# Attention's keys in four column groups, and the first queries' maxima in four row groups between the projections

## The chip, the cores and the metric

The kernel runs on one core of one Trainium2 chip, in one launch. The metric is the device time of that core in microseconds (us). Several executions are timed, and their median counts; one further execution is recorded by the hardware profiler, and every duration below comes from that one.

The core has five engines with queues of their own: PE multiplies matrices into PSUM, DVE and ACT work on vectors (ACT evaluates functions from tables that it has to load), POOL does slower vector work, and SP issues DMAs. They wait for each other through semaphores, and each takes its own instructions in order.

## What is computed

Four images of 256 channels and 64x64 pixels go through four layers, each on a group normalisation `_gn` of the running x and added back to it:

```
x = x + layer0(_gn(x))   # deformable 3x3 convolution
x = x + layer1(_gn(x))   # attention
x = x + layer2(_gn(x))   # deformable convolution, 16 groups
x = x + layer3(_gn(x))   # state-space (scan) layer
```

The change lies in layer 1:

```
q = xf @ Wq.T + bq            # 4096 pixels x 32
k = xf @ Wk.T + bk            # 4096 pixels x 32
v = relu(xf @ Wv.T + bv)      # 4096 pixels x 128
attn = softmax(einsum('bnc,bmc->bnm', q, k), axis=-1)
comb = einsum('bnm,bmd->bnd', attn, v) @ Wc.T + bc
out = concatenate([comb, v], axis=-1)
```

## The kernel before

The images are worked on one after the other, and the four layers of an image too; x stays in SBUF as two tiles of 128 channels by 4096 pixels (`x[:, 0]` and `x[:, 1]`). `layer1` works on chunks of 512 pixels (`NCH` is 8) and on tiles of 128.

First `scaled` writes the normalised x, `xn`, in sixteen pieces on DVE (L186), two for each chunk. Its statistics need a square root on ACT (L175), with a table load ahead of it.

Then comes the part that I call the opening. For every chunk j it projects values, keys and queries (L496 to L501; the weights of queries and keys are held four times side by side, so that a projection gives the same 32 numbers in all four groups of 32 partitions). A projection is two fp32 matmuls, for the two halves of the channels, and every fp32 matmul leaves two records in the profile. DVE makes v from pv (bias and relu, `vt`, L503). ACT copies 32 partitions of pk to `ka` (L505): chunk j goes to partitions 32(j % 4) on, columns 512(j // 4) on. ACT also copies pq to `qa` (L506). PE transposes vt in four pieces (L509), and ACT copies the result to `v` (L510). DVE adds vt to `x[:, 1]` (L516) and takes its statistics for the next layer (`note`, L152).

The softmax subtracts each query's maximum, which `greatest` (L441) finds ahead for a block of 512 queries. It is a generator. A block has 32 products of 128 queries with 512 keys: a query tile t, a key column block c and a partition group g, each over 32 rows of PE. It does n of them at a time as a unit, into n PSUM banks (L455), and one DVE instruction takes the maxima of the n (L465); then it yields. After the last unit it reduces to one maximum for each query (L468), splits that into three bf16 parts on ACT and DVE (L472 to L475), and yields; when it is called again it turns them with four matmuls (pmt, L479) and copies the rows to `mr` (L483), which `scores` needs.

For the first block, n is 2, and two buffers of two banks are used (L489). The opening calls the generator four times at the end of every odd chunk (L512 to L514), so two key chunks have just become ready, and 16 units stand in four bursts of four. The last two calls (L518 and L519) stand after the loop. For the other seven blocks n is 3, and units stand between the products of attention.

After the opening come 64 steps of attention. `scores` (L523) multiplies keys and queries for 4x128 keys and 512 queries in four row groups, adds the negative maxima with bf16 products (L531), and ACT takes the exponential (`e`, L544); POOL sums e (L546, L548) and `weigh` multiplies it with v (L555). `scores(0)` stands ahead of the first step. Its four PSUM banks (`l1s`) use the room that the opening's four banks `l1p` had.

The order on PE is written by hand (`manual_schedule`); on DVE, ACT and POOL the framework's scheduler orders the instructions, and it also puts in the waits. A later step of the build puts in ACT's table loads.

Of the kernel before, what the change touches and what calls it, by code (L numbers as in the profile page):

```python
# [9 lines left out]
F32 = mybir.dt.float32  # L10
I32 = mybir.dt.int32
BF16 = mybir.dt.bfloat16
AF = mybir.ActivationFunctionType
ALU = mybir.AluOpType
AX = mybir.AxisListType

P = 128
# [46 lines left out]
class Net:  # L64
# [346 lines left out]
    def layer1(self, x):  # L411


        nc, tc = self.nc, self.tc
        KT = NT // 4
        with tc.tile_pool(name="l1a", bufs=1) as pa, tc.tile_pool(name="l1b", bufs=2) as pb:
            xn = pa.tile([P, 2, N], F32, tag="xn1", name="xn1")
# [7 lines left out]
            wq, wk, wv, wc, bq, bk, bv, bc = self.l1w  # L425
            qa = pa.tile([P, N], F32, tag="qa", name="qa")
            ka = pa.tile([P, N // 4], F32, tag="ka", name="ka")
            v = pa.tile([P, NT, P], F32, tag="v", name="v")
# [12 lines left out]
            def greatest(qb, wide, n):  # L441


                m8 = pb.tile([P, 4, 8], F32, tag="m8", name="m8")
                m = m8.rearrange("p t m -> p (t m)")
                if n == 2:
                    units = [(t, c, g) for c in range(2) for h in range(2) for t in range(4) for g in (2 * h, 2 * h + 1)]
                else:
                    units = [(t, c, g) for t in range(4) for c in range(2) for g in range(4)]
                for u in range(0, 32, n):  # L450
                    now = units[u : u + n]
                    sc = wide("pm")
                    for i, (t, c, g) in enumerate(now):
                        r = slice(32 * g, 32 * g + 32)
                        nc.tensor.matmul(  # L455
                            sc[:, i, :],
                            qa[r, bass.ts(4 * qb + t, P)],
                            ka[r, bass.ts(c, 512)],
                            start=True,
                            stop=True,  # L460
                            tile_position=(32 * g, 0),
                        )
                    t, c, g = now[0]
                    at = 8 * t + 4 * c + g
                    nc.vector.tensor_reduce(m[:, at : at + len(now)], sc[:, : len(now), :], AX.X, ALU.max)  # L465
                    yield
                mx = pb.tile([P, 4], F32, tag="mx", name="mx")
                nc.vector.tensor_reduce(mx, m8, AX.X, ALU.max, negate=True)  # L468
                mp = parts[qb % 2]
                for i in range(3):  # L470
                    t3 = pb.tile([P, 4], BF16, tag="t3", name="t3")
                    nc.scalar.copy(t3, mx)  # L472
                    nc.scalar.copy(mp[:, :, :, i], t3.rearrange("p (t u) -> p t u", u=1).to_broadcast([P, 4, 4]))
                    if i < 2:
                        nc.vector.tensor_sub(mx, mx, t3)  # L475
                yield
                pt = wide("pmt")[:, 0, :]
                for t in range(4):
                    nc.tensor.matmul(  # L479
                        pt[:, bass.ts(t, P)], mp[:, t].rearrange("p g r -> p (g r)"), identb, start=True, stop=True  # L480
                    )
                mr = pb.tile([P, 512], BF16, tag="mr", name="mr")
                nc.vector.tensor_copy(mr, pt)  # L483
                rows.append(mr)

            with (
                tc.manual_schedule(engines={mybir.EngineType.PE}),
                self.banks(4, "l1p") as pone,
                self.banks(2, "l1w") as ptwo,  # L489
            ):  # L490
                pair = lambda name: ptwo.tile([P, 2, 512], F32, tag="pm", name=name)
                one = lambda name: pone.tile([P, 512], F32, tag="p", name=name)
                ahead = greatest(0, pair, 2)
                for j in range(NCH):
                    to = {}
                    for n, w in (("v", wv), ("k", wk), ("q", wq)):  # L496
                        to[n] = one("p" + n)
                        for ct in range(2):
                            nc.tensor.matmul(
                                to[n], w[:, ct, :], xn[:, ct, bass.ts(j, 512)], start=(ct == 0), stop=(ct == 1)  # L500
                            )  # L501
                    vt = pb.tile([P, 512], F32, tag="vt1", name="vt1")
                    nc.vector.tensor_scalar(vt, to["v"], bv, 0.0, ALU.add, ALU.max)  # L503
                    r = slice(32 * (j % 4), 32 * (j % 4) + 32)
                    nc.scalar.activation(ka[r, bass.ts(j // 4, 512)], to["k"][r, :], AF.Identity, bias=bk[r])  # L505
                    nc.scalar.activation(qa[:, bass.ts(j, 512)], to["q"], AF.Identity, bias=bq)  # L506
                    pt = one("pvt")
                    for i in range(4):
                        nc.tensor.transpose(pt[:, bass.ts(i, P)], vt[:, bass.ts(i, P)], self.ident)  # L509
                    nc.scalar.copy(v[:, 4 * j : 4 * j + 4, :].rearrange("p t c -> p (t c)"), pt)  # L510

                    if j % 2:  # L512
                        for _ in range(4):
                            next(ahead)  # L514
                    xs = x[:, 1, bass.ts(j, 512)]
                    nc.vector.tensor_add(xs, xs, vt)  # L516
                    self.note(x, 1, j)
                next(ahead)  # L518
                next(ahead, None)  # L519

            blocks = [{} for _ in range(NCH)]
# [82 lines left out]
            with (  # L604
                tc.manual_schedule(engines={mybir.EngineType.PE}),
                self.banks(1, "l1s") as pscore,
                self.banks(1, "l1m") as pwide,
                self.banks(1) as self.psum,
            ):

                def wide(name):
                    return pwide.tile([P, 3, 512], F32, tag="wide", name=name)

                scores(0)
                ahead = itertools.chain(*(greatest(qb, wide, 3) for qb in range(1, NCH)))
                steps = 0
                for s in range(NCH * KT):
                    qb, kt = s // KT, s % KT
                    e = blocks[qb]["e"]
                    if s + 1 < NCH * KT:  # L620
                        scores(s + 1)

                    for i in range(4):
                        if steps < 4 + 12 * (s + (i + 1) / 4) / KT:
                            next(ahead, None)
                            steps += 1
                        weigh(s, e[i // 2], i)
                    if qb and kt in (1, 2, 3):
                        (divide, spread, combine)[kt - 1](qb - 1)
                for do in (divide, spread, combine):  # L630
                    do(NCH - 1)
# [901 lines left out]
```

## Time and profile before

| | |
|---|---|
| median of 3 runs | 10302.39 us (10298.44 to 10305.17) |
| the profiled execution | 10256.01 us |
| its span in the trace | 10254.2 us |
| PE, DVE, POOL, ACT busy | 86%, 77%, 64%, 47% of the span |
| granted PE clock, mean | 0.957 |
| first image: first pv to the first e (L544) | 613.43 to 691.65 us |
| second image | 3165.61 to 3244.07 us |
| third image | 5705.30 to 5783.68 us |
| fourth image | 8247.20 to 8323.72 us |
| in 613.4 to 691.0 busy: PE, DVE, ACT, POOL | 72.66, 44.35, 17.18, 0.00 us |
| granted PE clock there | 0.87 |

A line of the timeline has the start and the length in us, the engine, the line of the kernel, the operation, its output and inputs, the shapes and the number of records that are merged; in brackets stands how long the engine idled before it, and what released it. `32*128` in a matmul is the part of the array that it uses, rows by columns. The end of a matmul is modelled, so a pass is better measured from start to start. In a table of windows each engine has its busy time and its number of instructions; then come the granted PE clock (1 is full speed), the share of the DMA engines and GB/s.

### The profile page before, as it was taken

The page shows a single profiled execution, that of the slowest core. Times are in us where ns is not written, and L with a number is a line of the kernel's source. Part 1 is how long each engine was busy: PE and PEld are TensorE (multiplying, and loading weights), DVE is VectorE, ACT ScalarE, POOL GpSimd, SP SyncE. Part 2 cuts the span into 40 slices and gives each one's busy share as a digit, 9 for nine tenths or more (in the row PEclk, how much of TensorE's full clock was granted, in tenths as well). Part 3 has the DMA queues.
Part 4 walks back from the last instruction along what each step waited for, and adds up shares of the span by engine and source line. Part 5 has one row for each costly group of instructions (what it writes and reads, how often), then busy time and mean ns, then how long its engine had stood idle before and what let it go on. Part 6 is the DMA issues. An engine that isn't in the chain of part 4 may idle for free. (4 is left out here: it accounts for less than half of the span.)

```text
span 10254.2 us, 89063 instructions
## 1 busy us (share of the span) xinstructions
PE 8808.1 (86%) x29193; PEld 4231.4 (41%) x29193; DVE 7924.0 (77%) x8975; ACT 4869.3 (47%) x7460; POOL 6576.2 (64%) x3768
## 2 busy tenths in 40 slices
PE   5889998888788999889878898988977899888997
PEld 3643333333464333333346433333335643333333
DVE  4864697999675469799968546989996854798998
ACT  3743224665473322566557332256655733216664
POOL 3746556787474655688757465568875736556886
PEclk8999999999899999999989999999998999999999
DMA  7930111111782011111179101111118910111111
GB/s 264 328 109 1 37 40 35 44 45 49 269 315 97 1 37 40 36 45 46 45 286 325 70 1 41 36 40 48 44 43 321 322 36 1 45 41 37 40 41 34
DMA packets 377894, 956.57 MB, mean 93 GB/s; under 512 B 34676, under 2 KB 107821, under 8 KB 375373
## 3 DMA queue, kind: packets, MB, share of 16 engines
q0 software_dynamic: 165888, 604.05, 16.4%
q1 hardware_dynamic: 211532, 346.73, 10.6%
q8 instruction: 234, 3.83, 0.2%
q14 instruction: 240, 1.96, 0.1%
HBM read 784.59 MB, written 92.32 MB: 86 GB/s over the span
## 5 line engine op out<-in xcount | busy, mean ns | idle before, releaser
L1378 DVE TENSOR_TENSOR_SCAN h<-da,carry,h 128x512 f32<-128x512 f32 x2048 | 2470.6, 1264 | 140.2 <-ACT da L1377 91.4
L1392 POOL TENSOR_TENSOR h<-h,cn 128x2048 f32<-128x2048 f32 x508 | 2300.2, 4528 | 41.3 <-POOL carry L1389 0.6
L1377 ACT ACTIVATE da<-delta,l3a 128x512 f32<-128x512 f32 x2048 | 1388.7, 689 | 1145.5 <-DVE h L1378 1143.7
L1290 PE MATMUL y<-h,ident 128*128 128x512 f32 x4096 | 1920.9, 613 | 1.9 <-POOL h L1395 0.9
L344 POOL DMA_INDIRECT g<-tab,idx x1152 | 1343.7, 1166 | 761.0 <-issue 349.8
L548 POOL TENSOR_TENSOR acc<-acc,e 128x1024 f32<-128x1024 f32 x480 | 1125.3, 2344 | 541.0 <-ACT e L544 519.8
L810 POOL TENSOR_TENSOR prod<-prod 128x512 f32<-128x512 f32 x640 | 945.9, 1499 | 745.9 <-DVE prod L802 716.7
L388 PE MATMUL pz<-cols,l0w 128*128 128x256 f32 x4608 | 1213.6, 410 | 173.6 <-DVE cols L377 80.2
L1290 PEld LDWEIGHTS y<-h,ident 128*128 128x128 f32 x4096 | 806.0, 197 | 1289.3 <-issue 1236.8
L1370 DVE TENSOR_TENSOR h<-du,bn 128x2048 f32<-128x2048 f32 x512 | 1157.9, 2261 | 26.6 <-PE bn L1298 26.2
L465 DVE TENSOR_REDUCE m<-pm 128x3 f32<-128x1536 f32 (+1 forms) x372 | 602.3, 1625 | 716.8 <-PE pm L455 715.1
L353 DVE SCALAR_TENSOR_TENSOR r<-g,wx,r 128x512 f32<-128x512 f32 x1152 | 857.7, 745 | 352.3 <-ACT r L352 262.4
L812 PE MATMUL pacc<-prod,ident 128*128 128x512 f32 x1920 | 960.7, 623 | 142.7 <-POOL prod L810 106.2
L388 PEld LDWEIGHTS pz<-cols,l0w 128*128 128x128 f32 x4608 | 895.2, 205 | 341.5 <-DVE cols L377 117.7
L555 PE MATMUL cx<-e,v 128*128 128x512 f32 x2048 | 1001.4, 616 | 0.0
L544 ACT ACTIVATE e<-sc 128x1024 f32<-128x1024 f32 x512 | 496.0, 1020 | 1032.8 <-PE sc L531 1032.8
L802 DVE TENSOR_TENSOR prod<-ring,A 128x1280 f32<-128x1280 f32 x640 | 932.7, 1477 | 19.7 <-DMA ring<-ring 13.1
L352 ACT ACTIVATE r<-g,wx 128x512 f32<-128x512 f32 x1152 | 826.3, 717 | 254.8 <-DMA g<-tab,idx 209.2
L370 PE MATMUL pt<-ident,acc 128*128 128x128 f32 x2304 | 428.3, 293 | 302.0 <-DVE acc L361 197.5
L1389 POOL COPY carry<-h 128x4 f32<-128x4 f32 x512 | 98.3, 192 | 807.0 <-DVE h L1378 795.0
L812 PEld LDWEIGHTS pacc<-prod,ident 128*128 128x128 f32 x1920 | 325.9, 190 | 702.1 <-POOL prod L810 459.7
L555 PEld LDWEIGHTS cx<-e,v 128*128 128x128 f32 x2048 | 352.2, 189 | 598.9 <-issue 596.3
(247 smaller groups left out, 11219.4 us busy)
## 6 DMA issues: line engine op xcount, KB each, us to landing
cn<-cd SPq DMA_DIRECT2D x512, 256.0 KB
tab<-vt SPq DMA_DIRECT2D x112, 640.0 KB
ring<-ring SPq DMA_DIRECT2D x288, 126.0 KB
ring<-ring SPq DMA_DIRECT2D x288, 124.0 KB
g<-tab,idx POOLq DMA_INDIRECT x1152
x<-in_x SPq DMA_DIRECT2D x64, 256.0 KB
out<-x SPq DMA_DIRECT2D x56, 256.0 KB
l0w<-in_l0w SPq DMA_DIRECT2D x4, 2304.0 KB
```

The costliest lines, as they stand in the source:

```text
L344: nc.gpsimd.indirect_dma_start(out=g[:], out_offset=None, in_=tab[:, :], in_offset=bass.IndirectOffsetOnAxis(ap=idx[:, t, k : k + 1], axis=0),
L388: nc.tensor.matmul(sums[m][:, ot, :256], wf[:, i, bass.ts(ot, P)], cols[m][:, i, :], start=(i == 0), stop=(i == 17),)
L548: nc.gpsimd.tensor_add(b["acc"], b["acc"], e)
L555: nc.tensor.matmul(blocks[qb]["cx"], v[:, 4 * (i + kt // 4 * 4) + kt % 4, :], e[:, bass.ts(i % 2, 512)], start=(kt == 0 and i == 0), stop= ...
L802: nc.vector.tensor_mul(prod[:, :, t, :].rearrange("p x (g c) -> p x g c", c=GC), ring[y // VR % 4][:, :, y % VR, :].rearrange("p x (g c) - ...
L810: nc.gpsimd.tensor_add(prod[:, i, :], prod[:, i, :], prod[:, i + 1, :])
L812: nc.tensor.matmul(pd, self.ident, prod[:, wx, :], start=(wy == 0 and wx == 4), stop=(wy == WIN - 1 and wx == 2))
L1290: nc.tensor.matmul(c["ys"][dc], self.ident, h[:, dc, :], start=False, stop=(n == DS - 1))
L1370: nc.vector.tensor_mul(h, c["du"], c.pop(("bn", n)).to_broadcast([P, 4, C]))
L1377: nc.scalar.activation(da, c["delta"][:, dc, :], AF.Exp, scale=al[:, dc, n : n + 1])
L1378: nc.vector.tensor_tensor_scan(h[:, dc, :], da, h[:, dc, :], carry[:, dc, n : n + 1], ALU.mult, ALU.add)
L1392: nc.gpsimd.tensor_mul(h, h, cn.to_broadcast([P, 4, C]))
```

## The change

The keys of four chunks are now projected together by `keys(c)`: eight matmuls in four column groups of PE, with one copy of the weights (`wk[:, ct, :32]`), each to 32 partitions of the same bank; one ACT instruction copies all 128 partitions to `ka`. It is called in chunks 0 and 1, after the query projection.

A unit of the first block now has four products, in four row groups, into one buffer of four banks; there are 8 units. The two orders of units become one. The units stand in the chunks from 1 on: behind the value projection from chunk 2, and before the transposes in chunks 1, 3, 5 and 6. The ninth step of the generator (split of the maxima) comes in chunk 6, and the last (pmt and mr) in chunk 7 between the value and the query projection. After the loop nothing of it is left to be done.

A tiny exponential of one column is added ahead of the loop. The built program's order on ACT has it, with its table load, ahead of the square root of L175 (numbered alike in both kernels); the lines of the changed kernel are those of the diff.

```
-                if n == 2:
-                    units = [(t, c, g) for c in range(2) for h in range(2) for t in range(4) for g in (2 * h, 2 * h + 1)]
-                else:
-                    units = [(t, c, g) for t in range(4) for c in range(2) for g in range(4)]
+                units = [(t, c, g) for t in range(4) for c in range(2) for g in range(4)]
...
-                self.banks(2, "l1w") as ptwo,
+                self.banks(1, "l1w") as pfour,
             ):
-                pair = lambda name: ptwo.tile([P, 2, 512], F32, tag="pm", name=name)
+                four = lambda name: pfour.tile([P, 4, 512], F32, tag="pm", name=name)
                 one = lambda name: pone.tile([P, 512], F32, tag="p", name=name)
-                ahead = greatest(0, pair, 2)
+
+                tiny = pa.tile([P, 1], F32, tag="tiny1", name="tiny1")
+                nc.scalar.activation(tiny, self.eps, AF.Exp)
+
+                def keys(c):
+
+                    pk = one("pk")
+                    for ct in range(2):
+                        for g in range(4):
+                            nc.tensor.matmul(
+                                pk[32 * g : 32 * g + 32, :],
+                                wk[:, ct, :32],
+                                xn[:, ct, bass.ts(4 * c + g, 512)],
+                                start=(ct == 0),
+                                stop=(ct == 1),
+                                tile_position=(0, 32 * g),
+                            )
+                    nc.scalar.activation(ka[:, bass.ts(c, 512)], pk, AF.Identity, bias=bk)
+
+                def project(n, w, j):
+                    to = one("p" + n)
+                    for ct in range(2):
+                        nc.tensor.matmul(to, w[:, ct, :], xn[:, ct, bass.ts(j, 512)], start=(ct == 0), stop=(ct == 1))
+                    return to
+
+
+                ahead = greatest(0, four, 4)
                 for j in range(NCH):
-                    to = {}
-                    for n, w in (("v", wv), ("k", wk), ("q", wq)):
-                        to[n] = one("p" + n)
-                        for ct in range(2):
-                            nc.tensor.matmul(
-                                to[n], w[:, ct, :], xn[:, ct, bass.ts(j, 512)], start=(ct == 0), stop=(ct == 1)
-                            )
+                    pv = project("v", wv, j)
                     vt = pb.tile([P, 512], F32, tag="vt1", name="vt1")
-                    nc.vector.tensor_scalar(vt, to["v"], bv, 0.0, ALU.add, ALU.max)
-                    r = slice(32 * (j % 4), 32 * (j % 4) + 32)
-                    nc.scalar.activation(ka[r, bass.ts(j // 4, 512)], to["k"][r, :], AF.Identity, bias=bk[r])
-                    nc.scalar.activation(qa[:, bass.ts(j, 512)], to["q"], AF.Identity, bias=bq)
+                    nc.vector.tensor_scalar(vt, pv, bv, 0.0, ALU.add, ALU.max)
+                    if j > 1:
+                        next(ahead, None)
+                    pq = project("q", wq, j)
+                    nc.scalar.activation(qa[:, bass.ts(j, 512)], pq, AF.Identity, bias=bq)
+                    if j < 2:
+                        keys(j)
+                    if j in (1, 3, 5, 6):
+                        next(ahead)
                     pt = one("pvt")
                     for i in range(4):
                         nc.tensor.transpose(pt[:, bass.ts(i, P)], vt[:, bass.ts(i, P)], self.ident)
                     nc.scalar.copy(v[:, 4 * j : 4 * j + 4, :].rearrange("p t c -> p (t c)"), pt)
-
-                    if j % 2:
-                        for _ in range(4):
-                            next(ahead)
                     xs = x[:, 1, bass.ts(j, 512)]
                     nc.vector.tensor_add(xs, xs, vt)
                     self.note(x, 1, j)
-                next(ahead)
                 next(ahead, None)
```

In the changed kernel L452 is the product of a unit, L462 its reduction, L492 the tiny exponential, L499 the matmul of the keys, L512 that of the projections, L531 the transposes, L548 the scores and L561 the exponential e.

## The prediction

> **What bounds the kernel now.** I read the page first: PE is busy 86% of the span, and the chain that ended last crosses all engines, so no engine sum decides an edit. The changed lines run once per image, between layer 1's normalisation and the first exponential of its attention; I call this the opening. So I asked for PE's timeline in the first image's opening (start us, duration us, engine, line, output<-input, records; an fp32 matmul leaves two records, one per pass).
>
> ```profile
> 613.43 3.75 PE L499 MATMUL pv<-xn,l 128*128 128x512 f32 x4 [2.52 <-DVE xn L186]
> 616.98 2.37 PE L499 MATMUL pk<-xn,l 128*128 128x512 f32 x4
> 619.18 1.88 PE L499 MATMUL pq<-xn,l 128*128 128x512 f32 x4
> ...
> 639.08 1.88 PE L499 MATMUL pv<-xn,l 128*128 128x512 f32 x4
> 640.80 1.88 PE L499 MATMUL pk<-xn,l 128*128 128x512 f32 x4
> 642.51 1.88 PE L499 MATMUL pq<-xn,l 128*128 128x512 f32 x4
> 644.23 0.60 PE L509 MATMUL pvt<-ident,vt 128*128 128x128 f32 x4
> 644.76 1.99 PE L455 MATMUL pm<-ka,qa 32*128 32x512 f32 x8
> 647.24 2.95 PE L455 MATMUL pm<-ka,qa 32*128 32x512 f32 x8 [0.49 <-DVE m L465]
> 650.12 3.78 PE L499 MATMUL pv<-xn,l 128*128 128x512 f32 x4
> 653.70 2.78 PE L499 MATMUL pk<-xn,l 128*128 128x512 f32 x4
> ```
>
> Ends overlap, so I count from start to start: a projection takes 1.71 us (640.80 to 642.51), the four transposes 0.43 to 0.53, and a burst of maxima 5.36 us (644.76 to 650.12), after which a projection takes 3.6 us. PE has almost no idle time, yet it is held up by the reductions and then by its clock. The windows (PE, PEld, DVE, ACT, POOL busy; then the granted clock) of a burst, of what follows, and of attention's first steps:
>
> ```profile
> 644.80:649.50 4.70, 4.20 (x17) 1.24 (x16) 3.44 (x3) 0.80 (x2) 0.00 (x0) 0.91 0.01 3
> 649.50:655.40 5.90, 5.90 (x8) 2.19 (x7) 2.79 (x4) 0.00 (x0) 0.00 (x0) 0.50 0.00 0
> ...
> 691.70:699.80 8.10, 6.15 (x21) 1.88 (x21) 1.76 (x1) 3.83 (x4) 5.72 (x4) 0.50 0.01 2
> 700.00:720.00 20.00, 16.74 (x80) 5.15 (x79) 10.54 (x6) 2.53 (x3) 6.82 (x3) 1.00 0.00 0
> ```
>
> The opening is on the path: PE, DVE and ACT all work on it alone, POOL is idle for 84.7 us before the first sum, and in the four images the time from the first pv to the first e (L544) is 78.2, 78.5, 78.4 and 76.5 us, 77.9 on average. The end of it, on ACT:
>
> ```profile
> 689.22 0.26 ACT L473 COPY mp<-t 128x16 bf16<-128x16 bf16 x1
> 689.50 1.28 ACT L544 ACT_TABLE_LOAD   x1
> 691.65 1.94 ACT L544 ACTIVATE e<-sc 128x1024 f32<-128x1024 f32 x2 [0.87 <-PE sc L531]
> ```
>
> The table load now lies under PE's bf16 products and costs nothing. Two prices for what the opening does not show come from other rows: column groups in layer 0 (timeline), and the two shapes of the reduction (groups by shape; busy us, mean ns of one).
>
> ```profile
> 76.98 15.66 PE L280 MATMUL po<-xnp,l 128*32 128x512 f32 x144
> ```
>
> ```profile
> L465 DVE TENSOR_REDUCE m<-pm 128x2 f32<-128x1024 f32 x16 | 19.0, 1220 | 11.6 <-PE pm L455 11.2
> L465 DVE TENSOR_REDUCE m<-pm 128x3 f32<-128x1536 f32 x7 | 12.3, 1757 | 14.7 <-PE pm L455 14.7
> ```
>
> **What the Trainium skill says.** "TensorEngine Tiling (Array Packing)", Performance Considerations: up to four column groups run beside each other where the stationary operand has at most 32 columns. The trace agrees: 18 groups of four take 15.66 us, 0.87 us a group, what one fp32 matmul takes (1.71 / 2 = 0.86). The same section says that tiling does not speed up the emptying of PSUM; here too, DVE's reductions pace the bursts. "TensorE: Matmul & The Clock Gate", Part 1: the clock is halved or full, set by how busy PE was in a free-running window of about 3.4 us; the trace shows 0.50 and 1.00 and nearly nothing between. "ScalarE: Activation LUTs", What ACT_TABLE_LOAD costs: 1283 ns plus a drain of about 1380 ns; here the load takes 1.28 us and the drain is not seen (the load at 689.50 was over long before e; the load before the square root at 610.99 is followed by it at 612.29), so I use 1.28.
>
> **The change part by part, per image.** *Keys:* eight projections pk (8 x 1.71 = 13.7 us) become two calls of keys, each two groups of four column matmuls, 2 x 2 x 0.87 = 3.5 us: PE loses 10.2 us. ACT loses eight 0.68 us copies and gains two; ACT has slack.
>
> *Maxima:* 16 units of two row groups become 8 of four. In attention a group of four starts at 707.95 and its successor at 708.91: 0.96 us; I take 1.0, so 8.0 us in place of four bursts of about 4.9 (20 us). A reduction over 2048 elements is not in the trace; the step from 1024 to 1536 is 0.54 us, so 1.76 + 0.54 = 2.30 us (between 2.2 and 2.5). Eight take 18.4 in place of 19.5. It starts 1.25 us after its unit does, as the three-wide ones do. There is now a single four-bank buffer where there were two of two banks, so a unit waits for the last reduction's end, and behind it on PE's queue wait the transposes and the next projections.
>
> *Order:* I walked the built program's order, in us from the first pv. DVE does vt, the addition to x and its statistics, 2.2 us per chunk (750 + 692 + 692 ns and gaps), before the next reduction. pv0 (half clock) ends at 3.55 and pq0 takes pk0's place, 5.75; keys 7.5, transposes 7.9, pv1 9.6, pq1 11.35, keys 13.1, unit 1 14.1, transposes 14.5, pv2 16.2. Keys wait for nothing: chunk 3 of xn is ready at 3.1, chunk 7 at 6.8. Reduction 1 ends at 16.6, so unit 2 ends at 17.65; pq2, transposes and pv3 21.5, unit 3 22.5, pq3 24.25. Its reduction waits on DVE for chunk 3's 2.2 us (21.7 to 23.9) and ends at 26.2: PE stands 2.0 us. Unit 4 27.25, pv4 29.4, a stall of 0.45 for reduction 4, unit 5 30.85, pv5 34.7, unit 6 35.7, pq5 37.4, a second stall of 2.0 us, unit 7 40.45, pv6 42.6, stall 0.45, unit 8 44.05, pv7 47.9. Reduction 8 ends at 47.5; the maximum and its split into three take 1.55 us, as between 687.93 and 689.48, so pmt starts at 49.2 (stall 1.3), pq7 ends at 51.3 and the transposes at 51.75.
>
> *Tail:* the old tail ran after everything (4.8 us of burst and 3.8 of split, pmt and mr); now pq7 and the transposes lie behind pmt, and mr is done before they are. But scores(0) lay inside the old burst, and now waits for the last copy of v (0.2 + 0.58) because its banks are reused: 52.55 to 53.5, its bf16 products 0.5 more, 54.0. And the order shows a loss: the tiny Exp at L492 stands ahead of the square root, which takes the table away again; so a load still stands before the first e, and it now comes behind the wait for the scores' end, where before it stood ahead of that wait. It costs 1.3 us: e at 55.3. The first e, and POOL's sum and scores(1) with it, wait for it. The new load at L492 costs nothing: it waits for layer 0's last matmul (606.6) and ACT idles until 610.99; without that cover it would cost 1.28. No DMA moves, and no queue of SP or POOL is passed.
>
> As a sum: PE 16 x 1.71 + 3.5 + 8.0 + 3.5 + 0.4 = 42.8, cold start 2.2, stalls 6.6, tail 3.6, together 55.2. DVE alone needs 8 x 2.2 + 18.4 = 36 from 6.8, so it is not the bound. Saved: 77.9 - 55.3 = 22.6, four times 90 us. Nothing later gives it back: attention keeps PE busy 19 to 20 of every 20 us from 720 on. The profiled execution took 10256.0 (span 10254.2, 1.8 around it); 90 off is 10166. The median of the runs is 10302.4, 0.45% more, so 10302.4 - 90 = 10212.
>
> **The rivals.** *Half clock after the two stalls of 2 us.* For: after bursts the clock fell, though PE had four units of 0.86 us in 4.7 us, but with half of its rows. Against: between 702.82 and 705.83 PE does a three-row unit and one full matmul, 1.7 us of 3.0, and stays at 1.00; in my worst window it is 1.4 of 3.4. One window of half clock costs 1.7 us: 4 x 2 x 1.7 = 14 us, 10226. *Attention's first steps keep the clock.* In the old ones PE ran at 0.50 until 699.8 after idling from 687; the first three-wide reduction starts 6.3 us after e and at full clock about 4.6. Up to 1.6 us an image, 6 in all: 10206. *The column groups do not overlap here* (the change doesn't do what it says): keys take 13.9 us, +10.4 each image: 10253; layer 0's row speaks against it. *Slower:* the clock stays at half through the opening, because units and stalls keep each window too idle. PE then needs 42.8 - 2.2 us more, some of it in the stalls: about 38, so 93 us in place of 78, four times 15: 10363. It decides from 22.6 us of extra PE time, that is when over half of the opening runs at half clock; full projections in every window speak against it.
>
> **How the numbers follow.** Main case 0.60, clock after stalls 0.20, kept clock 0.13, no overlap 0.04, slower 0.03. The main case's unknowns: a unit 0.9 to 1.15 us (8 x 4 gives -3 to +5 us), the reduction 2.2 to 2.5, met about six times on the path (-2 to +5), waits of 0.1 us at some 30 places (up to +12). With the two clock cases the range is 10188 to 10243. Faster by over 0.2% (20.6 us, about what a measurement tells from no change): 0.95; within: 0.02; slower: 0.03.
>
> **What would show it.** Right: from the first pv to the first e about 55 us; keys' eight matmuls within 1.8 us; reductions of 128x4 at 2.3 us; two PE waits of 2 us on L462 in chunks 3 and 5; clock 1.00 from the first window to the scores; a table load of 1.28 us between the scores and e. Wrong: windows at 0.50 in the middle, keys of 3.5 us each, or an attention loop that got longer by what the opening lost.

## The result, and the profile after

| | before | after |
|---|---|---|
| median of the runs of this comparison | 10298.66 us (5 runs, 10279.46 to 10305.17) | 10220.97 us (5 runs, 10214.20 to 10239.46) |
| ratio | | 0.9932, 95% interval 0.9916 to 0.9947 |
| the profiled execution, its span | 10256.0, 10254.2 us | 10214.2, 10212.3 us |

The change takes 77.7 us off the median, where 90 were forecast. The size of the opening is right to within 1 us an image. What is missing was given back behind attention, in a place that the prediction had looked past. These are PE's lines in the first image's opening after the change (start, duration, engine, line, output<-input, shapes, records; in brackets PE's idle time and what ended it):

```profile
626.45 3.75 PE L512 MATMUL pv<-xn,l 128*128 128x512 f32 x4 [2.52 <-DVE xn L186]
629.99 2.66 PE L512 MATMUL pq<-xn,l 128*128 128x512 f32 x4
632.59 1.92 PE L499 MATMUL pk<-xn,l 128*32 128x512 f32 x16
634.44 0.66 PE L531 MATMUL pvt<-ident,vt 128*128 128x128 f32 x4
...
640.32 1.14 PE L452 MATMUL pm<-ka,qa 32*128 32x512 f32 x8
641.39 0.66 PE L531 MATMUL pvt<-ident,vt 128*128 128x128 f32 x4
641.88 1.88 PE L512 MATMUL pv<-xn,l 128*128 128x512 f32 x4
643.96 1.14 PE L452 MATMUL pm<-ka,qa 32*128 32x512 f32 x8 [0.20 <-DVE m L462]
...
653.66 1.14 PE L452 MATMUL pm<-ka,qa 32*128 32x512 f32 x8 [1.50 <-DVE m L462]
...
666.91 1.14 PE L452 MATMUL pm<-ka,qa 32*128 32x512 f32 x8 [1.50 <-DVE m L462]
676.52 0.38 PE L476 MATMUL pmt<-identb,mp 128*128 128x128 bf16 x4 [0.84 <-DVE vt L520]
679.93 1.14 PE L548 MATMUL sc<-qa,ka 32*128 32x512 f32 x8 [0.82 <-ACT v L532]
```

From start to start, the keys of four chunks take 1.85 us (632.59 to 634.44) and a unit of four 1.07 (640.32 to 641.39). The brackets behind the first one are all that the view gives of PE's waits in the opening: 0.20, 1.50, 1.50, 0.84 and 0.82, together 4.9 us. The windows of the same opening (length; busy time of PE, PEld, DVE, ACT and POOL with the numbers of instructions; then the granted clock, DMA share, GB/s):

```profile
640.00:646.90 6.90, 6.70 (x33) 2.58 (x30) 5.31 (x5) 1.27 (x2) 0.00 (x0) 1.00 0.00 0
646.90:653.40 6.50, 5.26 (x21) 1.95 (x19) 5.41 (x5) 1.85 (x3) 0.00 (x0) 1.00 0.01 3
...
660.00:666.60 6.60, 5.41 (x21) 2.00 (x19) 5.61 (x5) 1.85 (x3) 0.00 (x0) 1.00 0.00 0
...
680.00:687.00 7.00, 3.64 (x27) 1.44 (x30) 0.00 (x0) 3.22 (x3) 3.17 (x2) 0.70 0.01 2
```

PE idles 1.2 us in two of these windows and keeps the full clock; before, the window behind a burst stood at 0.50. Only the window of the first e falls again. The reduction of four banks (groups by shape; busy us, mean ns of one), and the end of the opening on ACT:

```profile
L462 DVE TENSOR_REDUCE m<-pm 128x4 f32<-128x2048 f32 x32 | 73.0, 2280 | 20.0 <-PE pm L452 20.0
```

```profile
681.36 1.28 ACT L561 ACT_TABLE_LOAD   x1 [1.49 <-issue]
682.66 1.94 ACT L561 ACTIVATE e<-sc 128x1024 f32<-128x1024 f32 x2
```

The table load lies between the scores and the first e, as the built order had shown.

I cut both traces into stages (sums in us over the four images; the opening is from the first pv to the first e). The fourth row is the stage into layer 2: it ends where DVE forms its first product there, some 30 us after PE's first. The last image's layer 3 (983 and 982 us) is left out:

| stage | before | after | difference |
|---|---|---|---|
| layer 0 of the first image, to the first pv | 613.4 | 626.5 | +13.0 |
| openings | 311.6 | 223.6 | -88.0 |
| attention, to the end of layer 1's last sum | 1787.0 | 1787.6 | +0.7 |
| from there to DVE's first product of layer 2 (L802, L819) | 147.7 | 160.1 | +12.5 |
| from there to layer 3's first scan (L1378, L1395) | 1849.2 | 1846.9 | -2.3 |
| layer 3, and layer 0 of the next image, to its first pv | 4562.1 | 4585.5 | +23.4 |

The first and the last row belong to code that the change doesn't touch. They vary from kernel to kernel: in the six traces of the first runs, before among them, the last one's single images lie between 1514 and 1537 us, and the first row between 613 and 630. Because of them the two profiled executions lie only 41.8 us apart. I put nothing of them down to the change: in before_split, an experiment below that has none of it, the two rows add up to 5212.0 us (617.1 and 4594.9), as after the change (5211.9), where this trace of before has 5175.5. But the fourth row has the same sign in all four images (36.7, 36.5, 36.5 and 37.9 before; 40.9, 40.5, 40.4 and 38.4 after). There, DVE writes layer 2's normalised x (`xr`, L186) in twenty pieces while POOL clears the four rings (L690, L707). Before, in the first image: the pieces of a stretch of time (number; shortest, median and longest ns), POOL's memsets, and PE's first products:

```profile
L186 DVE TENSOR_SCALAR xr<-x,gm,rs x11: 456/531/2394, 1141.5 to 1149.7; 128x256 f32<-128x256 f32 x4, 128x384 f32<-128x384 f32 x4, 128x512 f32<-128x512 f32 x3
```

```profile
1137.79 9.03 POOL L690 MEMSET ring<- 128x2560 f32 x4
...
1142.60 1.19 PE L701 MATMUL pc<-l,xr 128*128 128x256 f32 x2 [1.69 <-DVE xr L186]
1144.80 1.19 PE L701 MATMUL pc<-l,xr 128*128 128x256 f32 x2 [1.01 <-DVE xr L186]
```

After:

```profile
L186 DVE TENSOR_SCALAR xr<-x,gm,rs x8: 394/470/4962, 1133.6 to 1140.6; 128x256 f32<-128x256 f32 x4, 128x384 f32<-128x384 f32 x4
```

```profile
1129.65 8.74 POOL L707 MEMSET ring<- 128x2560 f32 x4
...
1129.74 0.69 DVE L152 BATCH_NORM_STATS2 st<-x 128x6 f32<-128x512 f32 x1
...
1133.57 13.02 DVE L186 TENSOR_SCALAR xr<-x,gm,rs 128x256 f32<-128x256 f32 x20
...
1138.79 2.04 PE L718 MATMUL pc<-l,xr 128*128 128x256 f32 x4 [5.83 <-POOL l3a L974]
```

Before, the first piece took 0.83 us and the next two 2.39 each: they slipped in between memsets. After, the first piece, of 256 columns, takes 4.96 us and ends when the last memset does (1133.57 + 4.96 = 1138.53; 1129.65 + 8.74 = 1138.39). PE's first product of layer 2 (pc) waits for it: it starts 9.1 us after layer 1's end, where it started 4.8 us after it (with one more wait) before. In the fourth image it started late before the change too, after 6.9 us, behind a piece of 2.99 us. POOL's name in the bracket is that of the releaser that came last in the profile; POOL had only just got through its memsets too. And DVE's statistics of 0.69 us (L152) ran at their usual length beside the same memsets.

"SBUF — State Buffer", Who interferes with whom, in the Trainium skill, has a mechanism for this: VectorE (DVE) in a two-port mode and GpSimd (POOL) share one pair of ports as an exclusive lock, taken for a whole instruction, and tensor_scalar is among the instructions that can use that mode. The trace agrees in kind: a tensor_scalar of 512 columns takes 0.54 us (L186), faster than an addition of 512 columns with its 0.69 (L534), and it is held, while the statistics and three small operations on two inputs (gd, L169 to L171, 0.16 us each) are not. Whether that is the cause was to be tested.

### The profile page after: what moved, and what is told of

It reads as the page before. It is cut to its first block, busy times and chain, and to the rows that moved or that the text cites. A ratio compares the mean times of both kernels' runs of the same rounds, so it can differ in the third digit from the quotient of the medians.

```text
span 10212.3 us, 88995 instructions
## 1 busy us (share of the span) xinstructions
PE 8743.2 (86%) x29189; PEld 4199.5 (41%) x29193; DVE 7919.1 (78%) x8943; ACT 4862.0 (48%) x7444; POOL 6601.4 (65%) x3768
## 5 line engine op out<-in xcount | busy, mean ns | idle before, releaser
L1395 DVE TENSOR_TENSOR_SCAN h<-da,carry,h 128x512 f32<-128x512 f32 x2048 | 2470.5, 1264 | 136.5 <-ACT da L1394 88.1
L1307 PE MATMUL y<-h,ident 128*128 128x512 f32 x4096 | 1943.1, 619 | 4.0 <-POOL h L1409 2.8
L344 POOL DMA_INDIRECT g<-tab,idx x1152 | 1367.4, 1187 | 769.6 <-issue 362.7
L462 DVE TENSOR_REDUCE m<-pm 128x3 f32<-128x1536 f32 (+2 forms) x340 | 599.5, 1763 | 699.1 <-PE pm L452 699.1
L561 ACT ACTIVATE e<-sc 128x1024 f32<-128x1024 f32 x512 | 496.1, 1020 | 1028.5 <-PE sc L548 1028.4
L819 DVE TENSOR_TENSOR prod<-ring,A 128x1280 f32<-128x1280 f32 x640 | 932.9, 1477 | 16.1 <-DMA ring<-ring 9.6
```

The costliest lines, as they stand in the source:

```text
L344: nc.gpsimd.indirect_dma_start(out=g[:], out_offset=None, in_=tab[:, :], in_offset=bass.IndirectOffsetOnAxis(ap=idx[:, t, k : k + 1], axis=0),
L819: nc.vector.tensor_mul(prod[:, :, t, :].rearrange("p x (g c) -> p x g c", c=GC), ring[y // VR % 4][:, :, y % VR, :].rearrange("p x (g c) - ...
L1307: nc.tensor.matmul(c["ys"][dc], self.ident, h[:, dc, :], start=False, stop=(n == DS - 1))
L1395: nc.vector.tensor_tensor_scan(h[:, dc, :], da, h[:, dc, :], carry[:, dc, n : n + 1], ALU.mult, ALU.add)
```

## The experiments

The second column is the ratio to the kernel before, with its 95% interval; then come the means of four images, of the opening and of the stage from layer 1's end to DVE's first product of layer 2, in us, and the longest piece of `xr`. The kernels from keys_only on ran beside a kernel before of 10091 to 10093 us, since the stretch from the scan to the next image's first pv took 1464 to 1482 us there, in place of 1514 to 1537, and the first image's layer 0 some 570, in place of 613 to 630. So only ratios and stages are compared.

| kernel | ratio | opening | stage | longest piece |
|---|---|---|---|---|
| before | 1 | 77.9 | 36.9 | 2.39 (2.99 in one image) |
| after | 0.9932 (0.9916 to 0.9947) | 55.9 | 40.0 | 4.96 |
| after_split | 0.9906 (0.9883 to 0.9929) | 56.2 | 35.3 | 1.99 |
| after_stt | 0.9904 (0.9882 to 0.9925) | 56.2 | 35.3 | 0.61 of the first eight |
| before_split | 0.9989 (0.9982 to 0.9996) | 79.1 | 35.6 | 1.99 |
| tiny_late | 0.9907 (0.9888 to 0.9926) | 55.1 | 37.2 | 2.39 |
| keys_only | 0.9944 (0.9928 to 0.9961) | 66.3 | 36.9 | 2.39 |
| keys_wide | 0.9943 (0.9926 to 0.9960) | 65.4 | 37.2 | 2.39 |
| burst | 0.9964 (0.9952 to 0.9977) | 73.5 | 36.9 | 2.39 |
| defer | 0.9895 (0.9878 to 0.9911) | 53.9 | 37.9 | 2.39 (2.79 in one image) |
| after_again | 0.9910 (0.9894 to 0.9927) | 55.9 | 39.4 | 4.97 |
| tiny_out | 0.9906 (0.9889 to 0.9922) | 56.1 | 40.0 | 4.97 |
| best | 0.9896 (0.9880 to 0.9913) | 52.4 | 40.1 | 4.14 |
| best_stt | 0.9875 (0.9858 to 0.9891) | 52.8 | 35.1 | 0.61 of the first eight |

An interval is some 30 us wide, so a whole time can't tell edits of 5 or 10 us apart; the stages in the traces do.

### The stage given back

**after_split.** The ring memsets in five pieces each.

```
-                nc.gpsimd.memset(r, 0.0)
+                for u in range(WIN):
+                    nc.gpsimd.memset(r[:, u], 0.0)
```

> The changed kernel, but each of the four ring memsets of layer 2 (2560 columns, 2.2 us on POOL) is cut into five of 512 columns. Stage in question: from the end of layer 1's last sum to layer 2's first product, 36.7, 36.5, 36.5, 37.9 us before the change and 40.9, 40.5, 40.4, 38.4 after it; after the change the first piece of layer 2's normalised x on DVE takes 4.96 us, until POOL's memsets are done, where before the change the pieces slipped in between two memsets. Theory A (DVE's first piece is shut out while POOL's memsets run, and gets a turn only between two of them): shorter memsets give it a turn after about 0.5 us, the piece takes under 1.5 us, the stage falls to 34 to 37 us, the time by some 16 us, to about 0.9917 of the time before. Rival B (the piece waits for something else that the change made late, such as data or a semaphore): it still takes about 5 us and the stage stays at 40 to 41. Rival C (POOL keeps the turn from one memset to the next, however short they are): as B, the piece ends when the last memset does.

The stage fell to 35.3, 34.8, 36.4 and 34.9 us, 4.7 less than after the change. DVE's pieces and POOL's instructions in the first image:

```profile
L186 DVE TENSOR_SCALAR xr<-x,gm,rs x9: 437/753/821, 1125.8 to 1130.7; 128x256 f32<-128x256 f32 x4, 128x384 f32<-128x384 f32 x4, 128x512 f32<-128x512 f32 x1
```

```profile
1121.93 9.34 POOL L708 MEMSET ring<- 128x512 f32 x17
1131.25 0.53 POOL L975 TENSOR_SCALAR l3a<-l3a 128x64 f32<-128x64 f32 x1
1131.74 1.44 POOL L708 MEMSET ring<- 128x512 f32 x3
```

The first nine pieces take 0.44 to 0.82 us: each gets its turn at the end of a memset, as theory A has it. Only the tenth, which starts at 1131.47 behind POOL's other instruction, takes 1.99 us and is done only after the last of the three memsets that are left, as rival C has it. Rival B is out for this kernel: nothing but the sizes of POOL's instructions was changed.

**after_stt.** The first eight pieces in another form of DVE's instruction, beside the same memsets.

```
+                if slow > 0:
+                    slow -= 1
+                    by = rs[:, ct : ct + 1].rearrange("p (h u) -> p h u", u=1).to_broadcast([P, rows, W])
+                    nc.vector.scalar_tensor_tensor(to, xs, gm[:, ct : ct + 1], by, ALU.subtract, ALU.mult)
+                    continue
...
+                slow=8,
```

> The changed kernel, but the first eight pieces of layer 2's normalised x on DVE are made with scalar_tensor_tensor (x minus mean, times a broadcast 1/deviation) and not with tensor_scalar; the memsets on POOL stay as they are. In the traces, DVE's statistics and small additions run at their usual lengths while the same memsets run, and only this tensor_scalar is held up. Theory A, sharpened (only the faster form of the instruction, 0.54 us for 512 columns against 0.69 for a plain addition, has to share with POOL): the first piece takes 0.45 to 0.6 us beside the memsets, PE's first product of layer 2 starts 5 to 6 us after layer 1's end in place of 9.8, and the stage from layer 1's end to layer 2's first product falls from 40.5 to 35 to 37 us. Rival B (it waits for data or a semaphore): the piece is as late as in the changed kernel, and the stage stays at 40 to 41.

The stretch of time from layer 1's end (1130.46) in this kernel, first the pieces' durations, then the timeline:

```profile
L190 DVE SCALAR_TENSOR_TENSOR xr<-x,gm,rs x8: 479/548/613, 1134.3 to 1137.5; 128x256 f32<-128x256 f32 x4, 128x384 f32<-128x384 f32 x4
```

```profile
1130.41 8.73 POOL L714 MEMSET ring<- 128x2560 f32 x4
...
1134.33 3.79 DVE L190 SCALAR_TENSOR_TENSOR xr<-x,gm,rs 128x256 f32<-128x256 f32 x8
...
1135.08 2.04 PE L725 MATMUL pc<-l,xr 128*128 128x256 f32 x4 [1.34 <-DVE xr L190]
```

The memsets are as long as before, the first piece comes as late after them (3.92 us after the first one starts), and all eight are done in 3.79 us, while the memsets run. PE starts 4.6 us after layer 1's end. The ninth piece, a tensor_scalar again, shows the contrast in the same trace:

```profile
L192 DVE TENSOR_SCALAR xr<-x,gm,rs x12: 529/533/1389, 1138.0 to 1144.0; 128x512 f32<-128x512 f32 x12
```

It starts at 1138.04, while the last memset runs, and takes 1.39 us where the eleven after it take 0.53. So no data and no semaphore was late: it is the form of the instruction that is shut out, as theory A has it. The Trainium skill's same section says that an instruction with two inputs from SBUF is held only by a POOL instruction that reads SBUF, not by one that only writes; a memset doesn't read, and the eight ran freely.

**before_split.** The same split in the kernel before (diff as in after_split).

> The kernel before the change, with the ring memsets cut into five as in the run after_split. Theory A: there one or two pieces were held for 2.4 us each; they are held no longer, and the stage from layer 1's end to layer 2's first product falls from 36.6 to 34 to 36 us. The difference between this run and after_split is then the change without the accident in layer 2: 88 us from the four openings, a ratio near 0.9915 between them. Rival B: nothing moves here, the stage stays at 36.5, and the two kernels stay 76 us apart.

The stage fell from 36.9 to 35.6 us, and the time by 0.11%. So the kernel before paid for this meeting as well, by some 1.3 us an image. The openings of the two split kernels differ by 23.0 us an image, 92.0 in all, and their stages by 0.2 us an image; the difference of 12.5 us is gone. Their medians lie 92.9 us apart (10292.25 and 10199.32), a ratio of 0.9910 where 0.9915 was forecast.

**after_again.** The changed kernel once more.

> The changed kernel once more, unaltered, on the chip of this call. In its first trace the first piece of layer 2's normalised x took 4.96 us in all four images; in the traces of tiny_late, keys_wide, burst and defer, which differ from it in layer 1 alone, two pieces took 2.39 us each, as before the change. Theory A (which of the two happens is a matter of the moment at which the piece meets POOL's memsets, not of the change): the trace shows either pattern, and where it shows pieces of 2.39 us the stage from layer 1's end to layer 2's first product is 36.5 to 38 us, not 40.5, with openings of 56 us again. Rival D (the changed kernel's own timing into layer 2 leads to the long one each time): 4.96 us and 40 to 41 us again in at least three images.

Rival D holds: 4.97 us in all four images, a stage of 38.7 to 40.5, again. tiny_out has the long piece in all four images too, while tiny_late, keys_only, keys_wide and burst, with the same code for layer 2, never have it. So my theory that the moment decides fell: it goes with the build. What in the build decides stays open. In every image of after the first piece starts 3.92 us after the first memset, as in keys_wide, burst and two images of before; it has the same waits in before and after, and it stands at the same place of DVE's queue in after, tiny_late, keys_wide, burst and defer.

### The opening, part by part

**keys_only.** The kernel before with the keys of the change, and its bursts.

```
-                    for n, w in (("v", wv), ("k", wk), ("q", wq)):
+                    for n, w in (("v", wv), ("q", wq)):
...
+                    if j < 2:
+                        keys(j)
```

> The kernel before the change, with the keys alone made as in the changed kernel (two calls of keys, in chunks 0 and 1, one copy of the weights, column groups); the units of the maxima stay two wide and in their four bursts. Theory (the two parts of the change add up): the opening falls by the 10.2 us of the sum, from 77.9 to about 67.7, and the other 11.8 us of the change come from the units. Rival (the keys filled the time that the bursts' clock and reductions leave, or their removal lowers the clock further): the opening falls by under 7 us, to 71 or more.

The opening fell to 68.7, 68.6, 65.1 and 62.9 us, by 11.6 on average, where the theory had 10.2. The spread goes with the clock. Of this kernel's first and fourth image, the window at 18 to 24 us of the opening:

```profile
583.89:589.89 6.00, 6.00 (x13) 2.38 (x12) 3.63 (x5) 0.00 (x0) 0.00 (x0) 0.72 0.00 0
```

```profile
8047.54:8053.54 6.00, 6.00 (x20) 2.76 (x17) 4.04 (x5) 1.16 (x2) 0.00 (x0) 1.00 0.00 0
```

In the fourth image two of the three bursts that projections follow are not followed by half clock.

**keys_wide.** The change with full projections of the keys.

```
-                    pk = one("pk")
...
+                    for g in range(4):
+                        pk = project("k", wk, 4 * c + g)
+                        r = slice(32 * g, 32 * g + 32)
+                        nc.scalar.activation(ka[r, bass.ts(c, 512)], pk[r, :], AF.Identity, bias=bk[r])
```

> The changed kernel, but keys(c) makes its four chunks with four full projections (128 by 128, each 1.71 us) and four copies on ACT, in place of the column groups; the units stay four wide and between the projections. Theory (PE's work is the bound of the opening, so the column groups are worth their 10.2 us): the opening grows from 55.9 to 66 us. Rival (DVE's chain of reductions and of values hides part of it): it grows by under 7 us, to less than 63.

65.4 us, 9.5 more than after the change (10.2 expected). PE keeps the full clock and has the same two waits of 1.50 us. PE's own work is the bound, and the column groups are worth 9.5 to 11.6 us an image.

**burst.** The eight units in two bursts of four.

```
-                    if j > 1:
+                    if j == 7:
                         next(ahead, None)
...
-                    if j in (1, 3, 5, 6):
+                    if j in (2, 5):
+                        for _ in range(4):
+                            next(ahead)
+                    if j == 6:
                         next(ahead)
```

> The changed kernel, but the eight units of four stand in two bursts of four, in chunks 2 and 5, and not one by one between the projections. A unit's successor in a burst waits for the reduction: 1.25 us until it starts and 2.28 us of it, 3.5 to 3.6 us from unit to unit, where PE works 1.0. Theory (spreading the units is what hides the reductions, and keeps the clock): two bursts of 3 x 3.6 + 1.1 = 11.9 us in place of eight units of 1.07 and 4 us of waits, so 11 us more, and the granted clock falls to half after each burst for one or two windows of some 3 us, 1.5 to 3 us more each: an opening of 69 to 74 us. Rival 1 (the clock stays full after bursts of four full row groups): 65 to 68 us. Rival 2 (order does not matter, only the number of reductions): under 60.

73.5 us, within the theory's 69 to 74. PE in its second burst, and the projection behind it; and the window of 48 to 54 us:

```profile
618.35 1.14 PE L452 MATMUL pm<-ka,qa 32*128 32x512 f32 x8
621.91 2.09 PE L452 MATMUL pm<-ka,qa 32*128 32x512 f32 x8 [2.41 <-DVE m L462]
626.41 2.09 PE L452 MATMUL pm<-ka,qa 32*128 32x512 f32 x8 [2.41 <-DVE m L462]
630.91 2.09 PE L452 MATMUL pm<-ka,qa 32*128 32x512 f32 x8 [2.41 <-DVE m L462]
632.93 1.11 PE L534 MATMUL pvt<-ident,vt 128*128 128x128 f32 x4
633.84 2.75 PE L512 MATMUL pv<-xn,l 128*128 128x512 f32 x4
```

```profile
621.02:627.02 6.00, 2.70 (x12) 1.03 (x16) 3.12 (x2) 0.00 (x0) 0.00 (x0) 0.58 0.00 0
```

PE idles 2.4 us before each unit, the clock falls within the burst, and units grow to 2.1 us. Four-wide units with one buffer are thus no gain by themselves: with the same keys, this order is 7.2 us slower than keys_only with its two-wide, twice-buffered units, and 17.6 slower than the same units spread out. Whether two-wide units, spread out in the same way, would do as well was not run.

**tiny_late.** The tiny exponential reads v in chunk 5 and no longer stands ahead of the loop.

```
+                    if j == 5:
+                        tiny = pa.tile([P, 1], F32, tag="tiny1", name="tiny1")
+                        nc.scalar.activation(tiny, v[:, 20, 0:1], AF.Exp)
```

> The changed kernel, but the tiny exponential stands in chunk 5, reading a column of v, and not ahead of the loop; so the table of the exponential is loaded under chunk 5, after the square root and ahead of the split of the maxima. Theory (the load of 1.28 us before the first e is exposed, as the prediction has it, because it stands behind the wait for the scores): no load between the scores and e, the opening falls from 55.9 to 54.6 us, 5 us for four images. Rival (the wait for the products hides part of it, or the load in chunk 5 delays the split or a copy that PE waits for): the opening falls by under 0.4 us or gets longer.

The load is gone from the end:

```profile
684.32 0.39 PE L548 MATMUL sc<-mr,onesb 32*128 32x512 bf16 x4
684.80 1.94 ACT L561 ACTIVATE e<-sc 128x1024 f32<-128x1024 f32 x2 [1.50 <-issue]
```

From the start of the scores' last products to e it is 0.48 us, where the change had 1.77 (680.89 to 682.66): 1.29 saved, the theory. The opening is only 0.8 us shorter. The rest lies at its other end: the clock rises somewhat later in this trace, and the first keys start 6.1 to 6.4 us after the first pv, in place of 5.3 to 6.1; from there on the two run alike.

**tiny_out.** The change without the tiny exponential.

> The changed kernel without the tiny exponential ahead of the loop. Theory (as in the prediction, it costs nothing and gains nothing, since the square root behind it takes the table away again): the load of 1.28 us stays between the scores and the first e, the opening stays at 55.7 to 56.3 us. Rival (its own load delays the square root, or its place decides where the later load is put): the opening or the time ahead of the first pv changes by over 0.5 us an image.

The opening is 56.1 us, 0.2 more. The tiny exponential of the change gains nothing that shows.

**defer.** DVE's additions to x one chunk later: `settle()` makes those that are owed.

```
-                tc.manual_schedule(engines={mybir.EngineType.PE}),
+                tc.manual_schedule(engines={mybir.EngineType.PE, mybir.EngineType.DVE}),
...
-                    xs = x[:, 1, bass.ts(j, 512)]
-                    nc.vector.tensor_add(xs, xs, vt)
-                    self.note(x, 1, j)
+                    settle()
+                    owed.append((j, vt))
+                settle()
```

> The changed kernel, but on DVE the addition to x and its statistics of a chunk come one chunk later, behind the reductions that follow (DVE's order in the opening is written by hand for that). Theory (the two waits of 1.50 us on PE come from the addition and the statistics, 1.4 us, that stand ahead of a reduction): they shrink to under 0.5 us and the opening falls by 2 to 3 us, to about 53.5. Rival (DVE's total per chunk, 2.2 us of values and 2.3 per reduction, comes up again elsewhere, as a longer wait before the pmt or the scores): the opening falls by under 1 us or grows.

The opening fell to 53.9 us, by 2.0. The two waits are 0.50 us each:

```profile
599.34 1.14 PE L452 MATMUL pm<-ka,qa 32*128 32x512 f32 x8 [0.50 <-DVE m L462]
611.59 1.14 PE L452 MATMUL pm<-ka,qa 32*128 32x512 f32 x8 [0.50 <-DVE m L462]
```

### Together

**best** has the edits of after_split, defer and tiny_late; **best_stt** has those of after_stt, defer and tiny_late.

> The changed kernel with three edits together: memsets of layer 2 in pieces of 512 columns (after_split), additions to x one chunk later on DVE (defer), the tiny exponential in chunk 5 (tiny_late). Theory (their gains lie in different places and add up): openings of 53 us (55.9 - 2.1 - 0.8), a stage to layer 2's first product of 35.4 us, so 12 us from the openings and up to 21 us from the stage against the changed kernel's first trace: a ratio near 0.989 to the time before. Rival (the later additions delay the copy or the scores once the load is out of the way, or DVE meets the memsets anew): an opening of 54 us or more and a ratio above 0.991.

> As the run best, but the memsets stay whole, and the first eight pieces of layer 2's normalised x are made with scalar_tensor_tensor as in after_stt. Theory: openings of 53 us, a stage of 34.4 to 36.5 us, the same time as best within 0.1%. Rival (the slower form of the instruction costs more than the memsets' pieces did): 2 us or more longer a stage, 8 us in all.

The openings add up in both (52.4 and 52.8 us). The stage did not in best: its pieces met the memsets anew. The first pieces, and POOL, in the first image:

```profile
L186 DVE TENSOR_SCALAR xr<-x,gm,rs x5: 395/470/4137, 1078.3 to 1084.8; 128x256 f32<-128x256 f32 x4, 128x384 f32<-128x384 f32 x1
```

```profile
1074.39 7.91 POOL L717 MEMSET ring<- 128x512 f32 x17
...
1082.26 0.41 POOL L984 TENSOR_SCALAR l3a<-l3a 128x64 f32<-128x64 f32 x1
1082.64 1.44 POOL L717 MEMSET ring<- 128x512 f32 x3
```

The piece that started at 1078.31 got its turn after 4.14 us, when seventeen short memsets in a row were done and another kind of instruction came. That is rival C of after_split: shorter memsets help in one build and not in the next. The first piece starts 3.92 us after the first memset in both, so the moment of its start does not decide. (The ratio of best, 0.9896, is as forecast though its stage is not: whole times are too coarse for it.) Taking DVE out of the meeting held in both builds where it was tried, after_stt and best_stt: the stages are 35.3 and 35.1 us. The ratio of best_stt, 0.9875, is the lowest here, though its interval overlaps with that of defer; the forecast was the time of best within 0.1%, and it took 0.3% less. On the same chip the changed kernel took 10001.11 us and best_stt 9963.31, 37.8 less.

## Why the prediction was right, and where it was wrong

- **The sum of the opening** was 55.3 us, and the trace has 55.9 (saved: 22.0 of the forecast 22.6). Keys at 1.85 us for 1.74, units at 1.07 for 1.0, reductions at 2.28 for 2.30. How long the first products run at half clock (keys start 5.3 to 6.1 us after the first pv) differs from image to image; the openings lie between 55.7 and 56.2 us.
- **The waits** were given as 0.4 us before the second unit, 2.0 twice, 0.45 twice and 1.3 before pmt, 6.6 in all. In the first image they are 0.20, 1.50 twice, nothing that the view gives for the two of 0.45, and 0.84: 4.0 in all. The mechanism of the longest two is the one named, DVE's addition and statistics ahead of a reduction: defer takes 1.0 us off each. That the sum came out all the same is in part luck: the units (8 times 0.07), the keys (twice 0.11), the first products (6.1 us to the first keys for 5.75) and projections that meet a unit, which take 1.81 us (647.29 to 649.10) for the 1.71 of the sum, were each given too low.
- **The tail**: from pmt to the first e it took 6.1 us, as worked out (49.2 to 55.3). The exposed table load is confirmed by tiny_late, 1.29 us for the 1.3 given, and the worthless exponential by tiny_out.
- **The clock** stayed full after the waits, so the rival of half clock and the slower one are out. burst shows that the slower one's mechanism is real: with 2.4 us of idle time before each unit the clock falls. The column groups overlap, as keys_wide shows, so that rival is out too.
- **Attention's first steps** did not keep the clock: the window of the first e stands at 0.70, and attention took 0.2 us more an image.
- **The one step that failed** is the sentence "Nothing later gives it back: attention keeps PE busy 19 to 20 of every 20 us". Its reason holds for attention, and for nothing behind it. The stage into layer 2 took 3.1 us more an image, 12.5 in all: with the 88.0 of the openings that leaves 75.5 us, near the 77.7 of the medians. The profiled execution, worked out as 10166 us, took 10214.2: 12.5 us of that lie in this stage, and 36.4 in the two rows that the change doesn't touch. after_stt and after_split show that the loss is DVE's first piece waiting for POOL's memsets. It is a cost of this build and not of the change's idea: before_split and after_split differ by the openings alone. Nothing in the profile of before could give its size, but it did show pieces of 2.39 us beside a usual 0.46, and the range had no term for them. That it held the result all the same is owed to the width given for other unknowns.

The intervals of the whole times don't prove the 12.5 us by themselves: after_again, with the long piece, lies at 0.9910, as good as the kernels without it. The stages do.

## What to carry to other kernels

Where PE is paced by reductions, put single units between other products rather than in bursts: with four-wide units in one buffer, the order was worth 17.6 us an image here (burst against after), since it hides the reductions and keeps the clock; against the old two-wide bursts with the same keys, order and width together were worth 10.4. When an edit shortens one stage, look for instructions of very uneven length in the stages behind it, such as a DVE instruction of 0.46 us that sometimes takes 2.4; here they showed a meeting of two engines whose outcome a new build changed. And give the table load in front of a first function a place where its engine is idle, which took 1.29 us off the end of the opening (tiny_late); the function called ahead of another table's load gained nothing (tiny_out).

## What was not expected of the hardware

- A tensor_scalar on DVE of 256 columns took from 0.43 (after_split) to 4.97 us (after_again) beside POOL's memsets. When it was shut out, it lost its turn at two boundaries between memsets in a row (after), or at eight between short ones, until POOL came to another instruction (best). "SBUF — State Buffer", SBUF: two separate sides, in the Trainium skill, says that whichever starts first gets the pair for the whole instruction and the other fully blocks. Every run here agrees with the block; none shows who is served when a waiting DVE instruction meets POOL's next one, except that it is the same in nearly every image of one build and differs between builds, and in after_split between the first nine pieces and the tenth.
- scalar_tensor_tensor with a broadcast second operand took 0.48 us for 256 columns beside the same memsets, and tensor_scalar without company 0.39: the slower form costs 0.09 us and is not held.
